# A two-layer graph kernel: own variances, inverse roots and edge places computed in another way, with a redrawn order of work

## The chip, the cores and the metric

The kernel runs on one core of a Trainium2 chip. The metric is the device time of one launch in microseconds: the median of several runs. Engines are named as in the profile: PE is TensorE (matmul; PEld is its weight load), DVE is VectorE, ACT is ScalarE, POOL is GpSimd, SP is the queue that issues DMAs. All engines work in parallel, each takes its own instructions strictly in the order in which the program issued them, and semaphores hold an instruction back until its inputs are there and its output buffer is free.

## The reference

There are 32 graphs of 512 nodes with 128 features. About one in sixteen of the entries of each 512 x 512 adjacency matrix is nonzero, and every node has an edge to itself. Two layers follow each other:

```python
# layer 0
adj1 = adj + eye(N)
d = rowsum(adj1) ** -0.5
x = layernorm(x + (d[:, :, None] * adj1 * d[:, None, :]) @ (x @ weight) + bias)
# layer 1
m_j = x @ W1[:D];  m_i = x @ W1[D:]
pre = m_j[:, None, :, :] + m_i[:, :, None, :] + b1       # for each pair i, j
msg = gelu(layernorm(pre, g1, be1), exact)
agg = einsum('bijo,bij->bio', msg, adj)
upd = layernorm(concat([x, agg]) @ W2 + b2, g2, be2)
x = layernorm(x + upd)
```

Only pairs (i, j) with a nonzero adjacency entry contribute to `agg`. The variance of a pair's `pre` (with centred weights) is a sum of a square in i, a square in j and twice a product, so that a matrix of all pair variances comes out of a few matmuls.

## The kernel before, in words

**Sparse lists.** The kernel splits each 512 x 512 matrix into 16 blocks of 128 x 128 and each block's rows into two halves of 64. `layer0` computes layer 0 and then `key`: the pair variance where there is an edge, and about -1e30 where there is none (the bf16 `mask` is added by a matmul with `ident_h`, L421). VectorE finds with MAX8 and FIND_INDEX8 the eight largest entries of each half row (`lists`); the first four of each become "slots", handled by gathers. `more` removes these eight (MATCH_REPLACE8) and looks once more in the whole block. What is left over beyond the slots goes to shared places: `counts` counts the leftovers of each row and takes running sums by a matmul (`po`, L620), so that each row's leftovers occupy places from `first` + 1 to `last`; `spots` makes one-hot matrices `sj` (rows x places) from these; `sending` multiplies the rows' data by them; `picks` reads out the node numbers and variances of the shared places.

**A node's edge to itself** is handled apart. `layer0` zeroes the diagonal of the transposed adjacency `a_t` (L325, GpSimd), so that the mask says "no edge" there. The variances of these own edges come from a separate matmul, `pown` (L392, with the summed weights `w1s`), a Square on ScalarE (`own_sq`, L395) and four column sums on TensorE (`psq` over `own_sq`, L399). `own_edges` uses them.

**Inverse roots.** `factors` needs, for the 128 slot entries of each row, the standard deviation `sd` and its inverse `r`. ScalarE takes the Sqrt (L548), VectorE the reciprocal (L551). Sqrt needs another activation table than Gelu, so two table loads stand around it. `sd` is transposed on TensorE (`psd`, L556), split into three bf16 parts (L477 to L483), written to DRAM (`sd_d`, L564) and read back as `sd_rows` (L837). For the shared places `picks` takes a power of -0.5 on GpSimd (`rsqrt`, L231).

**c3.** `parts` computes `ac` and splits its second half into three bf16 parts `c3`: each part is a cast on ScalarE (L451) followed by a subtraction on GpSimd (L449).

**Units.** The pairs are computed in 20 units for each batch, named (t, q): four slots t = 0..3 with four row blocks q each, and four units with t = 4, 5 for the shared places. The unit order is (0,0) ... (2,3), (3,0), (3,1), (4,0), (3,2), (4,1), (3,3), (5,0), (5,1). Each unit passes through these stages:

- `gathers` (L818): VectorE compares node numbers that a DMA has broadcast, which gives one-hot rows `s`; `turned` transposes them by DMA (L826) into `mt`.
- `pairs` (L855 to L875): TensorE multiplies the one-hots with `c3`, `sd_rows` and, for shared places, `sj`, into one of two PSUM buffers `u`.
- `sums` (L881): VectorE adds `ac` and frees that buffer; only for slots. Units of shared places are read by ScalarE from PSUM.
- `messages` (L914): ScalarE, eight Gelu instructions with scale `r`.
- `weights` (L897, L901): GpSimd multiplies `mt` with the adjacency values, giving `sw`.
- `aggregate` (L928, L938): TensorE adds up `sw` times message in PSUM.

**Order.** There is no scheduler: the program issues everything in an order written out by hand. A batch has 40 steps (two per unit). At each unit the loop at L1022 issues pairs for two units, the aggregate of earlier ones, weights, sums and messages; at every step `prepare` issues pieces of the side work. `PLAN` holds, for each phase, the step (relative to the batch's first unit) at which each of its pieces (up to the next `yield`) is issued; negative steps lie within the units of the batch before. Within one step the phases go in the order finish, layer0, lists, factors, more, counts, spots, sending, picks, parts, own_edges. So `layer0` of a batch begins 44 steps ahead of its first unit. SP issues DMAs in the same order. PSUM has three banks (`ps`) for all the side work. `a_nat` (the loaded adjacency) and `key` share one buffer, so the next load waits until `more` has read `key` for the last time.

**spots before.** For each of eight pairs of blocks VectorE compares 258 place numbers with `last` (`up_to`, L647: 1 where the place number is at most `last`), TensorE takes differences between neighbouring rows with the matrix `step_down` (`pj`, L660), and VectorE copies the result from PSUM to `sj` (L655).

Of the kernel before, what the change touches and what calls it, by code (L numbers as in the profile page):

```python
# [8 lines left out]
F32 = mybir.dt.float32  # L9
BF16 = mybir.dt.bfloat16  # L10
# [7 lines left out]
EPS = 1e-5  # L18
# [14 lines left out]
    "layer0": [-44, -41, -39, -39, -38, -36, -36, -34, -31, -31, -31, -31, -30, -30, -29, -25, -25, -25, -24, -23, -20, -18, -17, -13],  # L33
    "lists": [-20, -20, -20, -20, -18, -18, -18, -18, -17, -13, -13, -13, -13, -13, -13, -13, -12, -11, -10, -9, -8],
    "parts": [-18, -13, -13, -9, -9, -9, -8, -7, -7],
    "factors": [-11, -11, -10, -8, -7, -7, -7, -7, -6],
    "more": [-20, -18, -11, -10, -9, -9, -8, -8, -8, -6, -6, -6, -6, -6, -6, -6, -6, -6],
    "counts": [-5, -5, -4, -4, -4],
    "own_edges": [-6, -4, 21, 29],
    "spots": [-3, -2, -2, -1, 0, 2, 3, 4, 5, 8],  # L40
    "sending": [9, 9, 9, 9, 9, 9, 9, 9, 9, 9, 9, 9, 9, 9, 9, 9, 9],
    "picks": [13, 15, 16, 17, 18, 20, 22, 23, 23, 23, 23, 23],
    "finish": [43, 48, 49, 50, 55, 57, 59, 61, 62, 70, 74, 75, 77],
# [22 lines left out]
def sparse_path(ctx, tc, x, adj, w0, b0, w1, b1, g1, be1, w2, b2, g2, be2, out, most, flag):  # L66
# [66 lines left out]
    step_down = const.tile([P, P], BF16, name="step_down")  # L133
    nc.gpsimd.memset(step_down, -1.0)
    nc.gpsimd.affine_select(
        out=step_down, in_=step_down, compare_op=ALU.is_equal, fill=0.0, base=-1, pattern=[[1, P]],
        channel_multiplier=-1,
    )
    nc.vector.tensor_add(step_down, step_down, ident_h)
# [27 lines left out]
    w1s = const.tile([P, P], F32, name="w1s")  # L167
    nc.vector.tensor_add(w1s, w1c[:, 0, :], w1c[:, 1, :])
# [60 lines left out]
    def rsqrt(dst, src):  # L229

        nc.gpsimd.tensor_tensor(dst, src, power[:, 0:1].to_broadcast([P, src.shape[-1]]), ALU.pow)  # L231

# [36 lines left out]
    def layer0(b):  # L269
# [80 lines left out]
        )  # L350
        yield
# [39 lines left out]
        pc = bank(f"pown_{b}")  # L391
        nc.tensor.matmul(pc, w1s, x1t, start=True, stop=True)  # L392
        yield
        own_sq = node.tile([P, N], F32, tag="own_sq", name=f"own_sq_{b}")
        nc.scalar.activation(own_sq, pc, AF.Square, bias=b1c_col)  # L395
        pa = bank(f"psq_{b}")
        for k, sq in enumerate((asq, own_sq)):
# [96 lines left out]
    def lists(b):  # L494
# [8 lines left out]
        def half(n, h):  # L503
            i0 = (n % C) * P + h * HALF
            return key[:, n // C, i0 : i0 + HALF]
# [821 lines left out]
```

## Time and profile before

| | us |
|---|---|
| median of three runs | 3031.48 (3030.92 to 3032.12) |
| the profiled execution, in all | 3032.46 |
| its span, first to last instruction | 3030.8 |
| weight loads (PEld) busy in the span | 2379.5 |
| mean granted TensorE clock | 0.988 |
| HBM traffic over the span | 56 GB/s |

A line of a group reads: line, engine, operation, output<-input by the program's names, shapes, number of instructions | busy us, mean ns of one | idle time of the engine just before them and what ended it. A line of waits reads: what waited <- what ended the wait: total us, number of times, longest. A line of windows reads: stretch, its length, busy time (and number of instructions) of PE, PEld, DVE, ACT, POOL, granted clock, busy share of the DMA engines, GB/s. A line for one source line reads: operation, number, duration ns min/median/max. Busy times of pipelined instructions are counted once where they overlap, so the mean of one instruction times the count can exceed the busy time.

The order of work within one batch can be seen on GpSimd and VectorE around the end of a batch. This is the timeline of GpSimd there (start, length, instruction, number merged, idle before):

```profile
1444.18 1.17 POOL L897 TENSOR_TENSOR sw<-mt,a_t 128x512 f32<-128x512 bf16 x1
1445.64 0.67 POOL L614 TENSOR_TENSOR a_t<-a_t,over 128x256 f32<-128x256 f32 x1 [0.29 <-DVE over L604]
1446.28 0.86 POOL L615 TENSOR_SCALAR a_t<-a_t 128x256 f32<-128x256 f32 x1
...
1449.00 1.04 POOL L464 TENSOR_TENSOR own_u<-own_u,own_r 128x512 f32<-128x512 f32 x1
1450.12 1.27 POOL L465 TENSOR_TENSOR own_u<-own_u,be_row 128x512 f32<-128x512 f32 x1
1451.34 4.54 POOL L901 TENSOR_TENSOR sw<-mt,sent 128x512 f32<-128x512 bf16 x4
```

### The profile page before, as it was taken

How to read it: one execution, taken by the hardware profiler on the slowest of the kernel's cores; microseconds unless marked ns; L12 is line 12 of the kernel's file. 1: busy time of each engine (PE TensorE's matmuls, PEld its weight loads, DVE VectorE, ACT ScalarE, POOL GpSimd, SP SyncE). 2: the span in 40 equal slices, each digit the busy share in tenths (PEclk: the TensorE clock that was granted, in tenths of full speed). 3: DMA queues.
4: the chain of work that ended last, by engine and by line, in shares of the span. 5: the costliest groups of instructions: out<-in, count | busy, mean ns of one | idle time of the engine just before them, and what ended most of it. 6: DMA issues, size and time to landing. Idle time of an engine off the chain costs nothing. (4 is left out here: it accounts for less than half of the span.)

```text
span 3030.8 us, 96573 instructions
## 1 busy us (share of the span) xinstructions
PE 2844.0 (94%) x35522; PEld 2379.5 (79%) x35713; DVE 2423.9 (80%) x9803; ACT 2560.8 (84%) x7873; POOL 2065.0 (68%) x2525
## 2 busy tenths in 40 slices
PE   4999999999999999999999999999999999999996
PEld 2788878878778788788788788788787887887875
DVE  6777888777988777988778988778887779887782
ACT  2888888888888888888888888888888888888885
POOL 3576766676776677766667766767666767766765
PEclk7999999999999999999999999999999999999998
DMA  2344443444443444443445433444434444434441
GB/s 58 73 94 99 103 96 78 94 98 99 98 98 77 97 91 106 98 91 82 90 93 112 96 82 81 98 99 101 96 78 96 97 100 98 98 77 97 88 92 45
DMA packets 593025, 276.14 MB, mean 91 GB/s; under 512 B 456112, under 2 KB 576048, under 8 KB 592544
## 3 DMA queue, kind: packets, MB, share of 16 engines
q1 hardware_dynamic: 592320, 269.41, 40.5%
q8 instruction: 284, 4.65, 0.6%
q14 instruction: 197, 1.61, 0.2%
q0 software_dynamic: 224, 0.46, 0.1%
HBM read 155.45 MB, written 13.63 MB: 56 GB/s over the span
## 5 line engine op out<-in xcount | busy, mean ns | idle before, releaser
L914 ACT ACTIVATE m<-m,r 128x128 f32<-128x128 f32 x4096 | 1263.7, 392 | 18.6 <-DVE m L881 18.5
L881 DVE TENSOR_TENSOR m<-u,ac 128x1024 f32<-128x1024 f32 x512 | 609.6, 1211 | 329.8 <-PE u L863 319.2
L897 POOL TENSOR_TENSOR sw<-mt,a_t 128x512 f32<-128x512 bf16 x512 | 616.4, 1224 | 18.0 <-DMA mt<-s 15.1
L928 PE MATMUL agg<-m,sw 128*64 128x128 f32 x8192 | 515.3, 277 | 3.1 <-POOL sw L897 2.8
L928 PEld LDWEIGHTS agg<-m,sw 128*64 128x64 f32 x8192 | 444.6, 137 | 69.9 <-issue 34.2
L855 PEld LDWEIGHTS <-s 64*128 64x128 bf16 x12288 | 364.8, 94 | 140.0 <-issue 98.2
L870 PE MATMUL u<-ac,sj 128*128 128x128 f32 x2048 | 441.4, 297 | 24.4 <-DVE m L881 18.4
L855 PE MATMUL u<-c,s 64*128 64x128 bf16 x12288 | 433.4, 218 | 13.3 <-DVE s L818 13.1
L243 POOL TENSOR_SCALAR ve_l<-mv_l 128x4 f32<-128x4 f32 x96 | 33.7, 351 | 468.3 <-DVE mv_l L240 468.3
L870 PEld LDWEIGHTS u<-ac,sj 128*128 128x128 f32 x2048 | 325.1, 192 | 32.6 <-DVE m L881 25.7
L872 PE MATMUL u<-c,s 128*128 128x128 bf16 x3072 | 339.5, 220 | 0.0
L672 ACT COPY sent<-pl 128x328 f32<-128x328 f32 x512 | 221.2, 432 | 112.8 <-PE pl L676 57.2
L901 POOL TENSOR_TENSOR sw<-mt,sent 128x512 f32<-128x512 bf16 x256 | 291.4, 1163 | 12.2 <-PE agg L938 8.5
L676 PE MATMUL pl<-a_t,sj 128*128 128x164 f32 x2048 | 297.8, 304 | 0.8 <-ACT aggt L766 0.8
L676 PEld LDWEIGHTS pl<-a_t,sj 128*128 128x128 f32 x2048 | 286.4, 190 | 7.7 <-ACT sent L672 6.6
L914 ACT ACTIVATE m<-u,r_s 128x128 f32<-128x128 f32 x1024 | 272.2, 379 | 8.0 <-PE u L875 5.9
L938 PEld LDWEIGHTS agg<-m,sw 128*128 128x128 f32 x2048 | 236.4, 192 | 52.8 <-issue 51.6
L872 PEld LDWEIGHTS <-s 128*128 128x128 bf16 x3072 | 259.9, 99 | 12.1
L938 PE MATMUL agg<-m,sw 128*128 128x128 f32 x2048 | 250.6, 278 | 0.1
L513 DVE FIND_INDEX8 idx<-top,key 128x8 uint32<-128x64 f32 x1024 | 210.1, 218 | 0.0
L581 DVE MATCH_REPLACE8 key<-top,key 128x64 f32<-128x64 f32 x1024 | 205.8, 208 | 0.0
L863 PE MATMUL u<-be_d,sd_rows 64*128 64x512 bf16 x1024 | 195.5, 378 | 0.0
(214 smaller groups left out, 5641.8 us busy)
## 6 DMA issues: line engine op xcount, KB each, us to landing
raw<-idx_d SPq DMA_DIRECT2D x256, 256.5 KB
raw<-idx_ds SPq DMA_DIRECT2D x64, 513.0 KB
a_nat<-in_adj_dram SPq DMA_DIRECT2D x32, 1024.0 KB
sd_rows<-sd_d SPq DMA_DIRECT2D x768, 12.0 KB
xs<-in_x_dram SPq DMA_DIRECT2D x32, 256.0 KB
out_dram<-o_sb SPq DMA_DIRECT2D x32, 256.0 KB
sd_d<-sd_p SPq DMA_DIRECT2D x256, 12.0 KB
mt<-s SPq DMA_TRANSPOSE x192
```

The lines of the kernel that those rows point to most:

```text
L513: nc.vector.max_index(idx[:, n - 1, h, :], top[:, n - 1, h, :], half(n - 1, h))
L672: nc.scalar.copy(sent[:, n - 1], pt[:, : SHARED * WIDE].rearrange("p (k w) -> p k w", w=WIDE))
L676: nc.tensor.matmul(pt[:, k * WIDE : (k + 1) * WIDE], sj[:, n, k * P : (k + 1) * P], at[:, n, :], start=True, stop=True,)
L855: nc.tensor.matmul(pu[:, h, c, :], s[halved(h), c, q * P : (q + 1) * P], c3[halved(h), k, c, :], start=(c == 0 and k == 0), stop=False,)
L870: nc.tensor.matmul(pu[:, h, c, :], place, st["ac"][:, q_h, 0, :], start=(c == 0), stop=False)
L872: nc.tensor.matmul(pu[:, h, c, :], s[:, c, q_h * P : (q_h + 1) * P], c3[:, k, c, :], start=False, stop=False)
L881: nc.vector.tensor_tensor(u.rearrange("p h c d -> p (h c) d"), pu.rearrange("p h c d -> p (h c) d"), bcast(state[b]["ac"][:, q, 0, :], 2 * C),
L897: nc.gpsimd.tensor_tensor(sw, mt[:, :, q, :], st["a_t"][:, q, :, :P], ALU.mult)
L901: nc.gpsimd.tensor_tensor(sw, mt[:, :, q_h, :], a, ALU.mult)
L914: nc.scalar.activation(m[:, h, c, :], u[:, h, c, :], AF.Gelu, scale=r[:, k : k + 1])
L928: nc.tensor.matmul(agg[halved(h), c, :], sw[0][:, c, halved(h)], m[:, h, c, :], start=(begin and c == 0), stop=(end and c == C - 1),)
L938: nc.tensor.matmul(agg[:, c, :], sw[h][:, c, :], m[:, h, c, :], start=False, stop=(end and h == 1 and c == C - 1),)
```

## The change

1. *Own variances from the keys' diagonal.* `pown`, `own_sq`, `w1s` and the second set of `psq` columns go. GpSimd sets the mask's diagonal to 0, so that `key` holds the own edges' variances there; GpSimd then multiplies the diagonal blocks of `key` by the identity and writes -1e30 onto the diagonal; VectorE reduces the product to `own_v`. In `lists` and `more` the four diagonal blocks are taken last (`seq`).
2. *Inverse roots by Newton.* A new `inverse_root` on GpSimd: a first guess from the number's bits, then three Newton steps of four instructions. It replaces Sqrt and reciprocal in `factors` (there `sd` is then the variance times `r`) and the power in `picks`. The power stays in the layer norms, `own_edges` and the degrees.
3. *c copies on GpSimd.* The three casts to `c3` move from ScalarE to GpSimd.
4. *Places by two comparisons.* `step_down` and `pj` go. `sj` is now (place > `first`) * (place <= `last`), one scalar_tensor_tensor on VectorE for each block, from `places_1` and `up_to`.
5. *Positions redrawn.* All of `PLAN` changes. `layer0` has two pieces more, `spots` one less.

```diff
 PLAN = {
-    "layer0": [-44, -41, -39, -39, -38, -36, -36, -34, -31, -31, -31, -31, -30, -30, -29, -25, -25, -25, -24, -23, -20, -18, -17, -13],
-    "lists": [-20, -20, -20, -20, -18, -18, -18, -18, -17, -13, -13, -13, -13, -13, -13, -13, -12, -11, -10, -9, -8],
-    "parts": [-18, -13, -13, -9, -9, -9, -8, -7, -7],
-    "factors": [-11, -11, -10, -8, -7, -7, -7, -7, -6],
-    "more": [-20, -18, -11, -10, -9, -9, -8, -8, -8, -6, -6, -6, -6, -6, -6, -6, -6, -6],
-    "counts": [-5, -5, -4, -4, -4],
-    "own_edges": [-6, -4, 21, 29],
-    "spots": [-3, -2, -2, -1, 0, 2, 3, 4, 5, 8],
-    "sending": [9, 9, 9, 9, 9, 9, 9, 9, 9, 9, 9, 9, 9, 9, 9, 9, 9],
-    "picks": [13, 15, 16, 17, 18, 20, 22, 23, 23, 23, 23, 23],
-    "finish": [43, 48, 49, 50, 55, 57, 59, 61, 62, 70, 74, 75, 77],
+    "layer0": [-44, -44, -41, -41, -41, -41, -39, -38, -38, -38, -37, -37, -35, -33, -33, -32, -32, -32, -32, -32, -30, -28, -27, -27, -21, -15],
+    "lists": [-30, -30, -29, -28, -28, -28, -26, -26, -23, -20, -20, -20, -19, -19, -18, -18, -18, -16, -16, -16, -16],
+    "parts": [-23, -18, -13, -7, -6, -5, -5, -5, -3],
+    "factors": [-12, -12, -12, -11, -9, -9, -8, -7, -5],
+    "more": [-18, -15, -11, -11, -11, -10, -7, -7, -7, -7, -6, -5, -5, -5, -5, -5, -5, -5],
+    "counts": [-5, -4, -4, -4, -4],
+    "own_edges": [5, 5, 9, 22],
+    "spots": [-4, -4, -4, -4, -4, -4, -4, 2, 4],
+    "sending": [1, 2, 4, 4, 4, 4, 4, 4, 4, 4, 4, 4, 4, 4, 4, 4, 4],
+    "picks": [4, 5, 7, 11, 11, 16, 17, 19, 19, 21, 21, 23],
+    "finish": [44, 45, 45, 47, 48, 51, 51, 53, 57, 69, 74, 80, 80],
 }
...
+    places_1 = const.tile([P, SHARED * P], BF16, name="places_1")
+    nc.vector.tensor_copy(places_1, place_w.rearrange("p k e -> p (k e)")[:, : SHARED * P])
...
+    def inverse_root(dst, src, key):
+
+        width = src.shape[-1]
+        guess = small.tile([P, width], I32, tag=f"guess{width}", name=f"guess_{key}", bufs=1)
+        nc.gpsimd.tensor_scalar(guess, src.bitcast(I32), -0.5, 1597463007.0, ALU.mult, ALU.add)
+        y = guess.bitcast(F32)
+        z = small.tile([P, width], F32, tag=f"z{width}", name=f"z_{key}", bufs=1)
+        for k in range(3):
+            nc.gpsimd.tensor_tensor(z, y, y, ALU.mult)
+            nc.gpsimd.tensor_tensor(z, z, src, ALU.mult)
+            nc.gpsimd.tensor_scalar(z, z, -0.5, 1.5, ALU.mult, ALU.add)
+            nc.gpsimd.tensor_tensor(dst, y, z, ALU.mult)
+            y = dst
...
+        own_m = mask.rearrange(blocks, i=P)[:, own, :]
+        nc.gpsimd.affine_select(
+            out=own_m, in_=own_m, compare_op=ALU.not_equal, fill=0.0, base=0, pattern=[[0, C], [1, P]],
+            channel_multiplier=-1,
+        )
...
-        pc = bank(f"pown_{b}")
-        nc.tensor.matmul(pc, w1s, x1t, start=True, stop=True)
-        yield
-        own_sq = node.tile([P, N], F32, tag="own_sq", name=f"own_sq_{b}")
-        nc.scalar.activation(own_sq, pc, AF.Square, bias=b1c_col)
+        yield
         pa = bank(f"psq_{b}")
-        for k, sq in enumerate((asq, own_sq)):
-            for q in range(C):
-                nc.tensor.matmul(
-                    pa[:, k * C + q : k * C + q + 1], sq[:, q * P : (q + 1) * P], ones[:, :1], start=True, stop=True
-                )
+        for q in range(C):
+            nc.tensor.matmul(pa[:, q : q + 1], asq[:, q * P : (q + 1) * P], ones[:, :1], start=True, stop=True)
...
+        own_k = key.rearrange("p q (c i) -> p (q c) i", i=P)[:, own, :]
+        picked = node.tile([P, C, P], F32, tag="t1", name=f"own_p_{b}")
+        nc.gpsimd.tensor_tensor(picked, own_k, bcast(ident, C), ALU.mult)
+        nc.gpsimd.affine_select(
+            out=own_k, in_=own_k, compare_op=ALU.not_equal, fill=NEG, base=0, pattern=[[0, C], [1, P]],
+            channel_multiplier=-1,
+        )
+        yield
+        own_v = small.tile([P, C], F32, tag="own_v", name=f"own_v_{b}")
+        nc.vector.tensor_reduce(own_v, picked, AX.X, ALU.add)
+        st["own_v"] = own_v
+        yield
...
-            nc.scalar.copy(c3[:, k], rest)
+            nc.gpsimd.tensor_copy(c3[:, k], rest)
...
+        seq = st["seq"] = [n for n in range(C * C) if n % (C + 1)] + list(range(0, C * C, C + 1))
...
-            nc.gpsimd.tensor_scalar(by_c[:, h], top[:, h, :, :, :SLOTS], 0.0, None, ALU.max)
-        yield
-        nc.scalar.activation(sd, sd, AF.Sqrt, bias=eps_t, scale=1.0 / D)
+            nc.gpsimd.tensor_scalar(by_c[:, h], top[:, h, :, :, :SLOTS], 0.0, 1.0 / D, ALU.max, ALU.mult)
+        nc.gpsimd.tensor_scalar(sd, sd, EPS, None, ALU.add)
         yield
         r = small.tile([P, n_r], F32, tag="r", name=f"r_{b}")
-        nc.vector.reciprocal(r, sd)
+        inverse_root(r, sd, f"{b}")
+        yield
+        nc.gpsimd.tensor_tensor(sd, sd, r, ALU.mult)
...
-            if k >= 2:
-                nc.vector.tensor_copy(
-                    sj[:, 2 * k - 4 : 2 * k - 2, :], pt.pop(k - 2).rearrange("p (n e) -> p n e", n=2)
-                )
-            if 1 <= k <= n_pairs:
-                pt[k - 1] = bank(f"pj_{b}_{k}")
-                nc.tensor.matmul(pt[k - 1], step_down, up_to.pop(k - 1)[:, :, : SHARED * P], start=True, stop=True)
+            if k:
+                before = up_to.pop(k - 1)
+                for n in range(2):
+                    at_n = 2 * k - 2 + n
+                    nc.vector.scalar_tensor_tensor(
+                        sj[:, at_n, :], places_1, first[:, at_n : at_n + 1], before[:, n, : SHARED * P],
+                        ALU.is_gt, ALU.mult,
+                    )
...
         r = small.tile([P, n_r], F32, tag="r_s", name=f"r_s_{b}")
-        rsqrt(r, ve)
+        inverse_root(r, ve, f"s_{b}")
```

## The prediction

> **What bounds the kernel now.** I read first the busy shares and the slices, then the time by windows, then TensorE's list of waits, then the groups by shape.
>
> ```profile
> PE 2844.0 (94%) x35522; PEld 2379.5 (79%) x35713; DVE 2423.9 (80%) x9803; ACT 2560.8 (84%) x7873; POOL 2065.0 (68%) x2525
> ```
>
> ```profile
> 1402.80:1494.50 91.70, 88.17 (x1112) 73.96 (x1118) 75.48 (x306) 79.86 (x248) 64.26 (x78) 1.00 0.43 94
> ```
>
> The second line is one batch (the same matmul of two successive batches stands 91.69 us apart), with busy time in the order PE, PEld, DVE, ACT, POOL. TensorE works 88.2 of 91.7 us at full granted clock. The others have 12 to 27 us to spare. TensorE's idle time is 3030.8 - 2844.0 = 186.8 us: by windows 46.4 of it lie in the first 92 us and 29.1 in the last 91, so 111 us over the 31 periods between, 3.6 each. As 32 x 91.69 = 2934.1, the span is 32 periods and 96.7 us.
>
> ```profile
> PE po L620 <- DVE count_h L612: 42.3, 31, 1.6
> PE pj L660 <- DVE sj L655: 22.3, 32, 1.7
> PE u L870 <- DVE m L881: 18.4, 30, 0.8
> PE pconv L357 <- DVE sj L655: 15.2, 30, 0.8
> PE u L855 <- DVE s L818: 13.1, 1, 13.1
> ```
>
> These are TensorE's longest waits (total, times, longest). The first four come once in each batch; the last is the start of the program. So time is gained only by what leaves TensorE's queue or shortens its waits. Whatever the other engines gain or lose counts only where TensorE comes to wait for it.
>
> **TensorE loses work.**
>
> ```profile
> L660 PE MATMUL pj<-up_to,step_down 128*128 128x512 bf16 x256 | 83.9, 387 | 24.7 <-DVE sj L655 22.3 <-DVE up_to L647 1.9
> L399 PE MATMUL psq<-ones,own_sq 128*128 128x1 f32 x256 | 33.6, 253 | 0.5 <-ACT own_sq L395 0.4
> L392 PE MATMUL pown<-x1t,w1s 128*128 128x512 f32 x64 | 33.0, 598 | 0.0
> ```
>
> All three groups go: 83.9 + 33.6 + 33.0 = 150.5 us. With pj go the 24.7 us idle before it and pconv's 15.2 us for a pj bank: 39.9.
>
> The two other waits sit in one chain, from the sum of unit (3,3) on VectorE to count_h. In the trace that sum starts 2.5 us after its matmuls end, as VectorE is still in "more". In the new order fewer "more" steps stand between the sums, and the transpose of xs (0.6 us) goes ahead of po, but a gather compare (1.2 us) goes ahead of count_h. Between keeping 42.3 + 18.4 = 60.7 us and losing them, I take half off: -30.
>
> **ScalarE** loses the two table loads of a batch (41.1 + 41.1), Sqrt 12.9, own_sq 21.9 and the c3 casts 59.0: 176 us, to 2385 or 74.5 a batch. On a spare engine that is worth nothing by itself.
>
> **VectorE** loses the sj copies (174.0) and the reciprocal (29.5). It gains 512 scalar_tensor_tensor of 128x256 from two SBUF inputs, a form that the trace lacks. Bounds are 0.344 us (the 128x128 form, L364) and 0.741 (128x512, L415); the nearest is tensor_tensor 128x256 from SBUF, 0.418 (L698), so 213.5 us. The reduce of own_v is like L713, 686 ns x 32 = 22. Net +32: 2456, 76.7 a batch. Hidden, as long as it is not in the wrong place (below).
>
> **GpSimd** gains, per batch:
> - the mask's and key's diagonal selects, as L325: 2 x 0.64, and the product own_p, as L446: 1.27. Together 2.55.
> - roots of 128x128: 13 Newton instructions, the EPS addition and sd*r, so 10 tensor_tensor and 5 tensor_scalar. The row of 128 elements on 32 partitions is 0.417 (L481); tensor_scalar lies between 0.249 (32 elements, L727) and 0.857 (256, L615), by proportion 0.51. 4.2 + 2.55, and 15 gaps of 0.08 between dependent instructions: 7.95.
> - roots of 128x32: 9 x 0.253 + 4 x 0.249 + 13 x 0.08 = 4.4 in place of the power, 5.44 + 0.08: -1.1.
> - three c3 copies of 128x512. Bounds are 0.285 (128x128, L599) and 1.16 (L449); I take the one-input row of that size, L325: 3 x 0.64 = 1.9.
>
> Sum +11.3: 64.5 to 75.8 us. Bounds: every 128- and 512-wide addition at the 1.27 us of a 512-wide tensor_tensor gives +25, so 90; every one at the smallest rows +6.
>
> **Where this meets TensorE's path.** (a) psd, a transpose in TensorE's order, now waits for GpSimd's whole block of roots (2 x 0.44 for the maxima + 7.95 = 8.8 us after the last "top"), before only for one activation. TensorE has the sums of units (2,2) and (2,3), pidx, and the pairs of (4,0) and (3,2) in between: 1.9 + 0.4 + 3.8 + 1.3 = 7.4 us, and about 0.9 of (3,1). Behind psd stand all later pairs. I take 0.5 us x 32 = 16, between 0 and 2 us (64).
>
> (b) The heavier one. Seven of the nine steps of "spots" now stand in one place, step -4, so VectorE runs 14 up_to compares (two take 0.51) and 12 of the new instructions in a row, 3.6 + 12 x 0.375 = 8.1 us, and the sums of (0,0) and (0,1) are queued behind. ScalarE's gelu of (0,0) waits for that sum, and s (L334) is queued behind the gelu, and TensorE's pconv waits for s. Counted from po, without a hindrance, sum (0,0) ends at 0.4 + 8.1 + 1.2 = 9.7 us, half the gelu and s at 12.1; TensorE comes to pconv after 2 x 1.5 (agg), 2.4 (pa), 1.6 (pairs), 1.0 (psup), 0.6 (pl) and 2 x 2.0 (agg) = 12.6. No wait, but 0.5 us of margin. GpSimd has sums of weights for (5,0) and (5,1), the c3 copy and the starts in the same stretch, 7.7 us. And VectorE and GpSimd hold each other up in this trace:
>
> ```profile
> L604 DVE TENSOR_SCALAR over<-a_t x32: 274/1245/1254, 69.1 to 2913.0; 128x256 bf16<-128x256 f32 x32
> ```
>
> The one execution beside an idle GpSimd took 274 ns. The other 31 overlap L897 on GpSimd and took 703 to 1254: the typical one begins 63 ns after L897 and ends 0.14 us after it. The other way round, ve_l (L243) has a median of 221 ns but 650 at most, while VectorE runs the two-input L707. The old sj copy has one PSUM input and never lengthened (676 to 691 ns) over 215 overlaps with GpSimd. If each of the 7.7 us on GpSimd delays the new instructions, sum and s move to 19.8 and pconv waits 7.2 us. If GpSimd slips between the up_to compares, 0. I take 1.7 x 31 = 53, bounds 0 and 223.
>
> The Trainium skill, "SBUF — State Buffer", section "SBUF: two separate sides", speaks against this edit: an instruction on VectorE with two SBUF inputs and a GpSimd instruction that reads SBUF exclude each other for the whole instruction. It agrees with the 1245 against 274 above (there in a fast mode of one input); whether the new form does the same no row shows. Taken strictly it puts (b) at its upper bound, and the time near 3055.
>
> (c) The start: psd stands at 56.7 us, and TensorE then idles 13.1 us for the first gather. The roots add some 7 us on the way of sd and the c3 copies stand behind them, partly inside that gap: +5, between 0 and 13.
>
> (d) The next batch's load. SP issues xs and a_nat (L273, L275) behind eight sd_d and six sd_rows issues, 3.7 + 2.4 us; in the trace a_nat is issued 1.7 us before po and used by the first mask 4.7 us after it (6.5 us of landing), and the first transposes of a_nat come 7 us after po. In the new order those stand 3 us after po. But the last cast of sd comes some 12 us before po (9 in the trace), and the last "more" frees the buffer 4.5 us before it, so the load would be there at -4.5 + 6.5 = 2.0. I take 0; without that cover 1.7 x 31 = 53.
>
> **Sum**, against the profiled execution's span: 3030.8 - 150.5 - 39.9 - 30 + 16 + 53 + 5 = 2884.4. That execution took 3032.46 in all; the median of the three runs, 3031.48, stands 0.7 above the span. Forecast 2885, a period of 87.1 us.
>
> **The rivals.**
> - *Nothing new waits:* (a), (b), (c) at 0: 2885 - 74 = 2811. For it: the positions leave margins, and three engines keep 10 us a batch. Against it: 0.5 us of margin at pconv. 15%.
> - *GpSimd becomes a second bound* at its upper costs: 96.7 + 32 x 90 = 2977. For it: the new instructions are short, and each waits for the one before. Against it: the 32- and 256-wide rows fit my prices. 18%.
> - *Slower:* the mutual exclusion at step -4 in full. Place: the 12 new instructions between po and the sum of (0,0); price 7.2 us in each batch: 2885 - 53 + 223 = 3055. It turns the change to a loss from (3031.5 - 2832) / 31 = 6.4 us of wait. For it: the row of L604. Against it: VectorE's up_to compares, 3.6 us, can lie beside GpSimd's work. 9%.
> - My forecast 58%.
>
> **Range.** 2825 to 2975: it leaves out the best part of the first rival, a few per cent of the second and all of the third. Faster or slower means by over 0.2%, some 6 us, about what a measurement of this kernel can tell from no change. The forecast and the first two rivals are all faster, and near the third's turning point little lies within 0.2%: 0.89, 0.02, 0.09.
>
> **What would show it.** TensorE busy near 2694; pj, pown and the second psq gone; no table load in the batches; ScalarE near 2385. GpSimd near 2425; 128-wide Newton instructions of 0.4 to 0.5 us; if over 0.8, the second rival. Waits of pconv for s (L341 of the changed kernel), and the duration of the two-input instruction (L682): near 0.4 it is free, near 1.3 the exclusion holds. psd waiting for sd by over 1 us a batch makes (a) too small. The prediction is wrong in its root if TensorE's idle time in the middle rises above 8 us a batch.

## The result and the profile after

| | us |
|---|---|
| before, median | 3031.2 (3030.83 to 3032.12) |
| changed, median of four runs | 3152.71 (3148.41 to 3155.73) |
| ratio | 1.040, 95% interval 1.038 to 1.042 |
| the changed kernel's profiled execution, span | 3153.4 |

The change makes the kernel 4% slower; the forecast was 2885 us. The busy times of the changed kernel:

```profile
PE 2840.0 (90%) x35137; PEld 2381.2 (76%) x35137; DVE 2628.0 (83%) x10058; ACT 2394.2 (76%) x7650; POOL 2364.6 (75%) x3579
```

ScalarE came out nearly as forecast (2385), GpSimd a little lower (2425 forecast), VectorE 172 us higher (2456). TensorE was to fall to 2694 and did not; its idle time rose from 186.8 to 313.4 us. One period of the changed kernel by windows (stretch, length, busy time of PE, PEld, DVE, ACT, POOL, clock, DMA share, GB/s):

```profile
1465.40:1560.90 95.50, 88.15 (x1098) 73.98 (x1098) 81.77 (x314) 74.71 (x240) 73.62 (x112) 0.98 0.40 90
```

A period has grown by 3.8 us, and the granted clock in it is no longer 1.00. TensorE's longest waits:

```profile
PE pconv L369 <- ACT s L341: 113.4, 31, 4.5
PE u L880 <- DVE m L906: 63.2, 66, 6.4
PE pidx L543 <- ACT idx_h L537: 30.8, 34, 5.7
PE pa L305 <- DMA a_nat<-in_adj_dram: 18.3, 13, 4.4
PE psd L576 <- POOL sd L571: 18.0, 14, 9.9
PE pcs L408 <- ACT at L400: 13.7, 31, 0.4
```

The waits of po, of pj and of the shared units' u are gone, as hoped. In their place stands one that the forecast knew by name, pconv for s, and a few that it had no term for. The groups (line, engine, shapes, number | busy us, mean ns | idle before):

```profile
L682 DVE SCALAR_TENSOR_TENSOR sj<-places,first,up_to 128x256 f32<-128x256 bf16 x512 | 351.2, 725 | 0.0
...
L369 PE MATMUL pconv<-s,a_t 128*128 128x128 f32 x1024 | 174.0, 350 | 117.2 <-ACT s L341 113.4 <-POOL a_t L332 3.8
...
L717 DVE TENSOR_SCALAR rank<-sent,place_k 128x64 f32<-128x64 f32 x64 | 43.8, 728 | 195.7 <-ACT sent L697 195.7
```

pconv waits, and then its 32 matmuls of a batch are slower too (350 ns a piece, 280 before). The new two-input instruction takes 725 ns on average, where 375 to 418 were put. The timeline around step -4 of one batch (start, length, engine, line, number merged, idle before) shows how the one makes the other:

```profile
1517.59 1.10 DVE L671 TENSOR_SCALAR up_to<-places,last 128x258 bf16<-128x258 bf16 x4
...
1518.62 1.22 DVE L682 SCALAR_TENSOR_TENSOR sj<-places,first,up_to 128x256 f32<-128x256 bf16 x2
...
1519.52 5.26 POOL L926 TENSOR_TENSOR sw<-mt,sent 128x512 f32<-128x512 bf16 x4
1519.87 0.60 DVE L671 TENSOR_SCALAR up_to<-places,last 128x258 bf16<-128x258 bf16 x2
...
1520.39 2.06 DVE L682 SCALAR_TENSOR_TENSOR sj<-places,first,up_to 128x256 f32<-128x256 bf16 x2
...
1525.62 0.87 DVE L682 SCALAR_TENSOR_TENSOR sj<-places,first,up_to 128x256 f32<-128x256 bf16 x2
...
1530.64 2.34 DVE L906 TENSOR_TENSOR m<-u,ac 128x1024 f32<-128x1024 f32 x2
1531.89 1.28 ACT L939 ACTIVATE m<-m,r 128x128 f32<-128x128 f32 x4 [5.62 <-DVE m L906]
1533.07 1.11 ACT L341 ACTIVATE s<-psup,dinv 128x128 f32<-128x128 f32 x4
...
1533.56 5.44 PE L369 MATMUL pconv<-s,a_t 128*128 128x128 f32 x32 [4.30 <-ACT s L341]
```

VectorE is on places from 1517.6 to 1530.6 without a break. A pair of two-input instructions takes 0.87 us when GpSimd runs little ones, and 2.06 while GpSimd's four sums of weights run (themselves 5.26, before 4.54). The sum of (0,0) and (0,1), then the gelu, then s are queued behind, and pconv comes last. Its 5.44 us were 3.81 before. The windows there (columns as above) show why:

```profile
1528.00:1532.00 4.00, 1.26 (x12) 1.07 (x10) 4.00 (x6) 0.11 (x1) 3.66 (x5) 1.00 0.52 134
1532.00:1536.00 4.00, 2.44 (x13) 2.47 (x14) 3.50 (x6) 4.00 (x16) 1.27 (x2) 0.74 0.01 2
1536.00:1540.00 4.00, 4.00 (x43) 3.82 (x44) 0.89 (x4) 2.26 (x8) 0.62 (x1) 0.83 0.01 4
```

After the idle stretch the clock is granted at less than full.

For the account below I laid the sequence of TensorE's matmul groups of all middle batches over one another. Each entry is us per period from a group's first start to the next group's first start, so a wait counts with the group before it (pconv's with "agg"); "pt" are the transposes of x, xs and agg; the last column is the best kernel of the experiments.

```
                 before   after   one operand (e3)   best (e16)
pj                 2.08    0.00    0.00               0.00
pown, own psq      1.87    0.00    0.00               0.00
pt                 2.94    1.57    1.51               1.50
u, all kinds      32.25   34.44   34.29              32.65
agg               23.54   27.77   23.86              24.00
pconv              3.65    5.23    3.57               3.57
all else          25.43   26.46   26.45              26.46
period            91.75   95.47   89.68              88.19
```

### The profile page after: what moved, and what is told of

Read it like the earlier page. It is cut to its first block, busy times and chain, and to the rows that moved or that the text cites. A ratio compares the mean times of both kernels' runs of the same rounds, so it can differ in the third digit from the quotient of the medians.

```text
span 3153.4 us, 96745 instructions
## 1 busy us (share of the span) xinstructions
PE 2840.0 (90%) x35137; PEld 2381.2 (76%) x35137; DVE 2628.0 (83%) x10058; ACT 2394.2 (76%) x7650; POOL 2364.6 (75%) x3579
## 5 line engine op out<-in xcount | busy, mean ns | idle before, releaser
L922 POOL TENSOR_TENSOR sw<-mt,a_t 128x512 f32<-128x512 bf16 x512 | 603.3, 1189 | 40.7 <-DMA mt<-s 39.7
L953 PE MATMUL agg<-m,sw 128*64 128x128 f32 x8192 | 531.3, 278 | 4.1 <-POOL sw L922 3.7
L953 PEld LDWEIGHTS agg<-m,sw 128*64 128x64 f32 x8192 | 452.7, 137 | 93.9 <-POOL sw L922 33.0
L880 PE MATMUL u<-c,s 64*128 64x128 bf16 x12288 | 435.7, 218 | 67.6 <-DVE m L906 63.2
L682 DVE SCALAR_TENSOR_TENSOR sj<-places,first,up_to 128x256 f32<-128x256 bf16 x512 | 351.2, 725 | 0.0
L926 POOL TENSOR_TENSOR sw<-mt,sent 128x512 f32<-128x512 bf16 x256 | 314.0, 1251 | 14.2 <-PE agg L963 8.4
L250 POOL TENSOR_SCALAR ve_l<-mv_l 128x4 f32<-128x4 f32 x96 | 21.4, 223 | 392.7 <-DVE mv_l L247 390.1
L701 PE MATMUL pl<-a_t,sj 128*128 128x164 f32 x2048 | 304.3, 304 | 0.0
L369 PE MATMUL pconv<-s,a_t 128*128 128x128 f32 x1024 | 174.0, 350 | 117.2 <-ACT s L341 113.4
L369 PEld LDWEIGHTS pconv<-s,a_t 128*128 128x128 f32 x1024 | 168.8, 262 | 122.4 <-issue 108.1
```

The lines of the kernel that those rows point to most:

```text
L369: nc.tensor.matmul(o, a_t[:, mc, c, :P], s[:, mc, :], start=(mc == 0), stop=(mc == C - 1))
L682: nc.vector.scalar_tensor_tensor(sj[:, at_n, :], places_1, first[:, at_n : at_n + 1], before[:, n, : SHARED * P], ALU.is_gt, ALU.mult,)
L701: nc.tensor.matmul(pt[:, k * WIDE : (k + 1) * WIDE], sj[:, n, k * P : (k + 1) * P], at[:, n, :], start=True, stop=True,)
L880: nc.tensor.matmul(pu[:, h, c, :], s[halved(h), c, q * P : (q + 1) * P], c3[halved(h), k, c, :], start=(c == 0 and k == 0), stop=False,)
L922: nc.gpsimd.tensor_tensor(sw, mt[:, :, q, :], st["a_t"][:, q, :, :P], ALU.mult)
L926: nc.gpsimd.tensor_tensor(sw, mt[:, :, q_h, :], a, ALU.mult)
```

## The experiments

Each ratio is to the kernel before, run beside it (3031.6 to 3033.9), with its 95% interval. "P", "X" and "L" are the theories that e1 names; "A", later, is the theory that grew out of X, and it had to be mended on the way.

### Which part costs what

**e1: the changed kernel at the positions of before** (two pieces for the longer layer0, one less for spots).

```diff
-    "layer0": [-44, -44, -41, ... -27, -27, -21, -15],
+    "layer0": [-44, -41, -39, ... -18, -17, -13, -13, -11],
-    "spots": [-4, -4, -4, -4, -4, -4, -4, 2, 4],
+    "spots": [-3, -2, -1, 0, 2, 3, 4, 5, 8],
```

> The changed code with the positions of the kernel before (two pieces of layer0 added at -13 and -11, spots spread over steps -3 to 8, lists shifted slightly so that each block is there when read). Theory P (the redrawn positions did the harm): TensorE's wait of pconv for s falls from 113 us to under 20, the sums' wait under 30; 2870 to 2960 us. Theory X (the two-input instruction and GpSimd exclude each other, and that costs wherever it stands): the instruction keeps a mean near 0.7 us; 2960 to 3060. Theory L (too much work moved to GpSimd and VectorE): above 3060 whatever the positions.

3372.92 us, ratio 1.113 (1.111 to 1.115). The redrawn positions are 220 us better for the new code than the old ones. What costs here is a wait of 10 us in each batch:

```profile
PE psd L576 <- POOL sd L571: 311.4, 32, 10.4
```

**e5: parts 1 to 3, with the old places on TensorE, at the positions of before.**

```diff
-                    nc.vector.scalar_tensor_tensor(sj[:, at_n, :], places_1, ...)
+                pt[k - 1] = bank(f"pj_{b}_{k}")
+                nc.tensor.matmul(pt[k - 1], step_down, up_to.pop(k - 1)[:, :, : SHARED * P], start=True, stop=True)
```

> The first three parts of the change (own variances, Newton roots, c copies) with the places as before (differences on TensorE) and the positions of before. TensorE loses pown and the second psq, some 60 us by their spacing. Theories P and X: 2950 to 3000 us, as nothing of these parts stands in TensorE's way; psd waits under 1 us a batch. Theory L: GpSimd's added 11 us a batch make TensorE wait for psd and for sw; 3040 or more.

3301.78 us, ratio 1.089 (1.087 to 1.091); psd waits 310.9 us in 32 times.

**e7: as e5, with the roots of before too** (parts 1 and 3 alone).

```diff
-        inverse_root(r, sd, f"{b}")
+        nc.scalar.activation(sd, sd, AF.Sqrt, bias=eps_t, scale=1.0 / D)
+        nc.vector.reciprocal(r, sd)
-        inverse_root(r, ve, f"s_{b}")
+        rsqrt(r, ve)
```

> Parts 1 and 3 alone (own variances from the keys' diagonal, c copies on GpSimd), with the roots and the places of before and the positions of before. Theory A (the 310 us that psd waited under these positions are the Newton roots' own): psd waits under 32 us in all, and the own variances' matmuls take some 60 us of TensorE with them: 2950 to 3000 us. Rival (own variances on the keys' way, or the copies on GpSimd, make the lists or the roots late): psd or another product waits over 150 us, 3100 us or more.

3053.9 us, ratio 1.008 (1.006 to 1.009). psd's wait is 1.8 us, so it was Newton's. But the 60 us for pown and its psq did not show: by starts they take 1.87 us out of a period, while agg takes 1.80 more (25.34) and po's, u's and agg's waits grow (u for m 32.3 us, 18.4 before; agg for sw 10.5, before 2.8). GpSimd's added work makes its sums of weights later, as the wait for sw shows. All waits together grow by 1.0 us a period; the rest of agg's 1.80 is no wait, its matmuls start further apart, and no run says why. Forecast had been 2950 to 3000.

**e4: part 4 alone, at the positions of before.** The same hunks of part 4, spots as in e1.

> The kernel before with part 4 alone (places by two comparisons on VectorE), at the positions of before, its nine pieces at steps -3 to 8. Theory A: the second comparison is costly only where VectorE has no slack, in a burst beside GpSimd; spread out, it costs VectorE time but no TensorE wait, and pj goes with its waits (24.7 + 15.2 us) and some 56 us of TensorE: 2930 to 2990 us, L682's counterpart at 0.6 to 0.8 us mean, pconv waiting under 0.5 us a batch. Rival: the comparison excluded beside GpSimd makes VectorE late wherever it stands: 3050 us or more, u waiting for m over 100 us. Between the two neither stands alone.

3102.54 us, ratio 1.023 (1.021 to 1.025), L682's counterpart at 809 ns on average, u for m 63.6 us. A expected a gain: it fell here, the rival held. pconv does not wait (2.2 us). The dear instruction costs even when spread.

At the positions of before, then, parts 1 and 3 cost 21 us, Newton's roots 248 (e5 less e7), the places 71 (e1 less e5; 70 alone): together the 340 by which e1 is slower. None of the three gains there.

**e9 and e11: the changed kernel with part 4 undone; and with the roots undone too.** Redrawn positions, the code as in e5 and e7, ten pieces of spots:

```diff
-    "spots": [-4, -4, -4, -4, -4, -4, -4, 2, 4],
+    "spots": [-4, -4, -4, -3, -3, -2, -1, 0, 2, 4],
```

> The changed kernel with part 4 alone undone (places by one comparison and TensorE's difference again, ten pieces at steps -4, -4, -4, -3, -3, -2, -1, 0, 2, 4), all else as redrawn. Theory A (the second comparison of two SBUF operands is what the changed kernel loses by): pconv's wait for s falls from 113 to under 25 us, pj comes back with 84 us busy and some waits; from the 2972 us of the kernel with one comparison of one operand, plus pj's two us a batch and up to one of waits: 3035 to 3075 us, so 80 to 115 us under the changed kernel. Rival (places at step -4 are late whoever makes them): 3120 us or more, with pconv or pl waiting.

> As the kernel with part 4 undone, and the inverse roots undone too (square root on ScalarE, reciprocal on VectorE, power on GpSimd), the positions redrawn. Theory A (Newton's roots cost 250 us at the positions of before because psd is due too soon after the lists, and the redrawn positions give them that time): within 25 us of the kernel with part 4 undone. Rival (Newton's roots cost GpSimd time that is dear wherever they stand): this kernel is 60 us or more faster than that one.

e9: 3161.33 us, ratio 1.042 (1.040 to 1.044); e11: 3316.28, ratio 1.096 (1.092 to 1.099). In e9 pconv's wait for s fell as expected (2.6 us; another 11.2 are for the PSUM bank that the copy to sj frees), but pj came back dearer than in the kernel before, where 24.7 us were idle ahead of it:

```profile
L689 PE MATMUL pj<-up_to,step_down 128*128 128x512 bf16 x256 | 98.5, 405 | 72.2 <-DVE up_to L676 37.0 <-ACT x_t L302 31.0
```

So the undoing is no clean test of part 4: at step -4 the places are late by either way. In e11 both theories fell: the roots of before are 155 us worse at the redrawn positions. More than half of it shows behind one of VectorE's waits:

```profile
DVE r L575 <- ACT sd L572: 112.4, 32, 3.6
```

The reciprocal stands in the same step as ScalarE's square root, VectorE waits 3.5 us for it in each batch, and the sums behind it make u wait (80.8 us). Newton on GpSimd alone crosses no engine. The same part loses 248 us at one set of positions and wins 155 at the other.

### The places at step -4

**e3: the second comparison with one SBUF operand.**

```diff
-                    nc.vector.scalar_tensor_tensor(
-                        sj[:, at_n, :], places_1, first[:, at_n : at_n + 1], before[:, n, : SHARED * P],
-                        ALU.is_gt, ALU.mult,
+                    nc.vector.tensor_scalar(
+                        sj[:, at_n, :].rearrange("p (k e) -> p k e", k=3), places, first[:, at_n : at_n + 1],
+                        None, ALU.is_gt,
```

> The changed kernel with its positions, but sj is made by one comparison with one SBUF input (place > first); the second comparison's result is left out of sj. Theory X: the instruction takes under 0.45 us in mean beside GpSimd, the run of twelve at step -4 shortens from 13.0 to some 7.5 us, pconv's wait for s falls under 20 us; 3000 to 3060 us. Theory P: a run of 24 instructions ahead of the sum is too much in itself; pconv's wait stays above 60; above 3090. Theory L: gain under 30 us, as VectorE loses under 5 us a batch.

This kernel leaves the comparison with `last` out of sj, so it serves for its time alone. 2972.32 us, ratio 0.981 (0.979 to 0.982): 180 us less than the changed kernel. pconv waits 2.7 us and its matmuls are at 281 ns again. The second comparison in the changed kernel and here (three durations: least, median, most):

```profile
L682 DVE SCALAR_TENSOR_TENSOR sj<-places,first,up_to x512: 466/480/1495, 81.8 to 3057.9; 128x256 f32<-128x256 bf16 x171
...
L682 DVE TENSOR_SCALAR sj<-places,first x512: 459/469/482, 77.1 to 2875.6; 128x258 f32<-128x258 bf16 x171
```

Where GpSimd is idle beside them, both take 470 ns (median of 14 and of 22). So the edit takes away the hold, not a dearer operation; a mean of 725 ns with a median of 480 says that the hold falls on a part of the 512 only.

**e2: the changed kernel, pieces of spots one to a step.**

```diff
+    "spots": [-4, -3, -2, -1, 0, 1, 2, 3, 4],
```

> The changed kernel with one line of positions altered: the nine pieces of spots stand at steps -4 to 4, one each, in place of seven at -4. Theory P: sum (0,0) is no longer behind twelve two-input instructions, pconv's wait for s falls from 113 us to under 30, TensorE's clock stays at full there (pconv back from 174 us busy to about 125); 3010 to 3070 us. Theory X: mean of the two-input instruction still near 0.7 us, pconv's wait falls by no more than half; 3080 to 3120. Theory L: within 20 us of 3153.

3061.21 us, ratio 1.009 (1.007 to 1.011). pconv's wait falls to 6.4 us, but u now waits 104.5 us for m: the dear instruction moved, and holds up other sums.

**e6, e8 and e10: the first comparison into PSUM.** e6 at the changed positions; e8 with the first five picks later as well; e10 with the pieces spread, and both comparisons of a pair in one piece.

```diff
-                up_to[k] = node.tile([P, 2, n_places], BF16, tag="up_to", ...)
+                up_to[k] = bank(f"up_to_{b}_{k}").rearrange("p (n e) -> p n e", n=2)
```

> The changed kernel and its positions; only, the first comparison writes its result to PSUM, so that the second reads one operand from SBUF and one from PSUM; the same sum is computed. Theory A (two SBUF operands are held up by GpSimd's, and that makes the burst at step -4 late): the second comparison falls from 725 ns to 420 to 520 ns on average, pconv's wait for s from 113 us to under 25 us, and the time to 2960 to 3010 us, near the 2972 us of the kernel with one comparison of one operand. Rival (what made that one fast was the operation itself, or PSUM banks are now short): the comparison stays over 650 ns or TensorE waits for banks, 3060 us or more.

> As the kernel with the PSUM operand, and the first five picks at steps 8, 9, 10, 12 and 14 in place of 4, 5, 7, 11 and 11. If VectorE's wait for sent (rank at step 4, 196 us in all in the changed kernel) is what makes m late for u, u's wait for m falls from some 55 to under 25 us and the time by 25 to 60 us against that kernel: 2920 to 2970 us. If that wait of VectorE lies beside work that TensorE has in hand anyway, the two agree within 10 us.

> The changed kernel with the first comparison into PSUM, both comparisons of a pair in the same piece (so that VectorE holds one bank at a time and gives it back within the piece) and the pieces one to a step from -4. The same sum is computed. Theory A (second comparison at some 475 ns, no bank kept from TensorE): pa's wait for sj falls from 220 us to under 20 us, pconv's for s stays under 15 us, u's for m is under the 105 us of the kernel that only spread the pieces; 2960 to 3010 us. Rival (TensorE has too few banks even so, or VectorE's load near step 0 itself costs the time): pa or u waits over 100 us, 3040 us or more.

e6: 3300.32, ratio 1.088 (1.086 to 1.090). The two-operand instruction, one operand in PSUM, is no longer held up (three durations: least, median, most):

```profile
L684 DVE SCALAR_TENSOR_TENSOR sj<-places,first,up_to x512: 460/473/480, 83.6 to 3201.0; 128x256 f32<-128x256 bf16 x171
```

But of the three PSUM banks of the side work VectorE now keeps two, and TensorE waits for them:

```profile
PE pa L307 <- DVE sj L684: 220.3, 32, 7.8
PE pl L703 <- DVE sj L684: 39.9, 32, 5.2
```

e8 is worse still, 3368.25 (ratio 1.111, 1.109 to 1.113): u's wait for m rises from 13.9 to 36.2 us and agg's for sw from 3.7 to 15.8, the opposite of what was expected. e10: 3028.35, ratio 0.998 (0.997 to 0.999), pa still waits 37.9 us for a bank. The operand was mended, the banks took it back.

**e12 and e17: the same sum by two instructions with one SBUF operand each,** at the changed positions. A place's distance from the first one is written in bf16; its bits, read as uint16, are compared with the bits of the count, so a negative distance is a large number. e12 makes the distance by two operations into a tile with gaps; e17 by one, without gaps.

```diff
-                        places, last[...], None, ALU.is_le,
+                        places, first[...], 1.0, ALU.subtract, ALU.subtract,
...
-                    nc.vector.scalar_tensor_tensor(...)
+                    nc.vector.tensor_scalar(
+                        sj[:, at_n, :].rearrange("p (k e) -> p k e", k=3), before.bitcast(U16)[:, n, :, : n_places // 3],
+                        bits[:, at_n : at_n + 1], None, ALU.is_lt,
```

> The changed kernel and its positions, the same sum, by two instructions with one SBUF operand each: the place's distance from the first one (bfloat16), and that distance's bits read as an unsigned 16-bit number and compared with the bits of the count (a negative distance is then a large number). Theory A (the loss is the second SBUF operand): the second instruction takes 400 to 500 ns beside GpSimd as alone, pconv's wait for s is under 15 us, and the time is 2960 to 2990 us, the one of the kernel with one comparison of one operand. Rival (that kernel was fast because work was missing, or 258 columns of any instruction in a burst are too many): 3040 us or more.

> As the distance kernel at the changed kernel's positions, its first instruction with one operation (the first place plus one is made once a batch) and a result without gaps. Theory A: the first instruction comes to 330 to 400 ns as in the kernel with one comparison of one operand, the stretch at step -4 to 8.3 to 9.5 us, pconv's wait under 20 us, the time to 2960 to 3000 us. Rival (subtraction, not the form, makes that instruction long): it stays at 500 ns or more and the time at 3090 to 3130 us.

e12: 3111.66, ratio 1.028 (1.024 to 1.031); e17: 3077.2, ratio 1.014 (1.012 to 1.015). Neither comes to e3's 2972. The durations of e12:

```profile
L673 DVE TENSOR_SCALAR up_to<-places,first x512: 281/308/1329, 78.6 to 3000.7; 128x258 bf16<-128x258 bf16 x171
...
L685 DVE TENSOR_SCALAR sj<-up_to,bits x512: 456/466/477, 79.6 to 3004.7; 128x258 f32<-128x258 uint16 x171
```

and of e17:

```profile
L675 DVE TENSOR_SCALAR up_to<-places,second x512: 330/340/351, 79.2 to 2981.7; 128x258 bf16<-128x258 bf16 x171
...
L686 DVE TENSOR_SCALAR sj<-up_to,bits x512: 340/351/1418, 80.3 to 2984.5; 128x258 f32<-128x258 uint16 x171
```

In each kernel one instruction keeps its time within 7%, and the other, which has only one SBUF operand as well, is stretched to over four times. The stretched one is the faster form of its kind: alone it takes 293 ns where the steady form of the first instruction takes 340, and 342 where the steady form of the second takes 466. "Two SBUF operands" was too narrow a name for what is held up.

**e18: the changed kernel, two of the seven pieces moved to steps -2 and 0.**

```diff
+    "spots": [-4, -4, -4, -4, -4, -2, 0, 2, 4],
```

> The changed kernel, with two of the seven pieces at step -4 moved to -2 and 0; instructions and operands as they were. Theory A (all of the stretch of places at step -4 beyond some 9.5 us reaches TensorE, whatever makes it long): the stretch falls from 13.1 to some 9 us (18 of 26 instructions), pconv's wait for s from 113 to under 15 us, its product's 174 us back to under 130 us, and the time to 2980 to 3030 us. Rival (two SBUF operands cost TensorE wherever they stand, as in the kernel with pieces one to a step, 3061 us): u's wait for m grows to 100 us and the time is 3050 us or more.

3161.1, ratio 1.043 (1.041 to 1.044), pconv waits 124.6 us. The edit did not do what I took it to do: no sum stands on VectorE between steps -4 and 0, so the stretch stayed at 13.1 us. It rules nothing out.

The kernels together give the relation that the expectation named. "Stretch" is the median, over the middle batches, of VectorE's time from the first comparison after `first` to the last one before the next sum; the wait is pconv's for s, divided by 31 batches:

| | stretch, us | wait, us a batch | pconv, ns each |
|---|---|---|---|
| e16 | 7.7 | 0.1 | 280 |
| e3 | 8.3 | 0.1 | 281 |
| e14 | 8.4 | 0 | 280 |
| e2 | 8.9 | 0.2 | 278 |
| e17 | 11.4 | 2.5 | 323 |
| e12 | 12.3 | 2.8 | 332 |
| changed | 13.1 | 3.7 | 350 |

Up to some 9 us the stretch is hidden; beyond that pconv waits, in three kernels with three forms of instruction. It is not one for one: in the changed kernel the seven batches with a stretch of 11.7 us make pconv wait 0.7 to 2.1 us, the 23 with 13.1 us 3.7 to 4.5.

### The waits that the forecast did not price, and a better kernel

**e13, e14, e15: from e12.** e13 copies idx_h one step earlier; e14 also spreads the pieces; e15 is e13 with the first three picks later.

```diff
-    "lists": [... -18, -18, -18, -16, -16, -16, -16],
+    "lists": [... -18, -18, -18, -17, -16, -16, -16],
     e14:
+    "spots": [-4, -3, -2, -1, 0, 1, 2, 3, 4],
     e15:
-    "picks": [4, 5, 7, 11, 11, 16, ...
+    "picks": [6, 7, 8, 11, 11, 16, ...
```

> As that one, with the copy of idx_h one step earlier (-17 in place of -16) than its product. If the redrawn positions' same step for both is what makes TensorE wait for it (30.8 us, about 1 us a batch), that wait goes and the time falls by 15 to 40 us. Rival (ScalarE's copy at -17 holds up m there, or TensorE waits elsewhere instead): within 10 us of it.

> As that second one, with the pieces of the places one to a step from -4 to 4. If with one SBUF operand the burst at -4 is harmless, this brings nothing or costs up to 30 us (VectorE is then loaded up to step 4, where sent is made from the last places: pl waits for sj); if the burst still costs, it is 20 us or more faster.

> As the kernel with idx_h earlier, and the first three picks at 6, 7 and 8 in place of 4, 5 and 7. If VectorE's wait for sent at step 4 is what makes u wait for m (54.8 us with one comparison of one operand), that wait falls under 30 us and the time by 15 us or more; rival: the picks' later parts then crowd VectorE or GpSimd and the time stays within 10 us or rises.

e13: 3121.17, ratio 1.029 (1.026 to 1.031), no gain over e12: pidx's wait falls from 30.9 to 20.3 us, but agg then waits 15.4 us for m, the gelu of ScalarE, which makes the copy. The rival held. e14: 2989.71, ratio 0.986 (0.984 to 0.988), 131 us under e13. e15: 3080.99, ratio 1.016 (1.013 to 1.020), 40 us under e13, and u's wait for m goes from e13's

```profile
PE u L886 <- DVE m L912: 53.1, 65, 4.3
```

to e15's

```profile
PE u L886 <- DVE m L912: 7.4, 18, 4.3
```

So that wait was made by the picks at step 4, where VectorE stands waiting for `sent` (196.7 us in e13, 124.9 in e15) with the sums queued behind.

**e16: e17's instructions, the pieces spread, the first three picks later.**

> The distance kernel with its short first instruction, the pieces one to a step from -4 to 4, idx_h's copy at -16 again and the first three picks at 6, 7 and 8. If what each brought adds up (2990 us for the spread one, some 40 us by the picks, a few by the shorter first instruction): 2930 to 2965 us. Rival (u's wait for m is then VectorE's load around steps 0 to 4, which the picks don't change): 2975 us or more.

2927.36 us, ratio 0.965 (0.963 to 0.966), against the kernel before; 225 us under the changed one.

```profile
PE 2769.2 (95%) x34946; PEld 2327.0 (79%) x35137; DVE 2588.1 (88%) x10121; ACT 2392.9 (82%) x7650; POOL 2354.7 (80%) x3579
```

VectorE is busy for 40 us less than in the changed kernel, and the difference is mostly where its work stands.

## Why the prediction was wrong

By periods, the forecast's terms that recur in each batch make -4.7 us (its sum over 32, without the start), measured were +3.7. The difference of 8.4, times 32, is the 268 us.

**The removal (-150.5 - 39.9, or -5.95 a period): mechanism right, size a little off.** pj, pown, the own psq and the waits in "pt" took 5.3 us out of a period. A group's busy time holds pipeline overhang that lies beside its neighbours: by starts the three groups were 3.95 us a period, 126 us, not 150.5. Missing: 0.6 a period, 20 us.

**Term (b), pconv behind the places (+53): the step that failed first.** Place, chain and mechanism were as the prediction put them; the margin was better than put (stretch of about 9 us, forecast 8.6). The size failed: "8.1 us" for the stretch holds for a form that is not held up (e3: 8.3) and not for this one (13.1). (The instruction alone takes 470 ns, not the 375 put, but so does e3's, so that is not what makes the difference.) The wait is 113.4 us. And the prediction had no price for what comes after a wait: pconv's matmuls at less than full clock, 1.6 us more a period. Together 5.1 a period in place of 1.7: 3.5, or 110 us. e3, which has the same positions without the hold, shows it: it is 180 us faster.

**"I take half off: -30", and nothing else: the second failed step, as dear.** The waits of po and of the shared u did go. But the forecast looked for new waits only where the code changed, and four came with the redrawn positions: u for m 63.2 us behind the picks at step 4 (shown by e13 against e15, in e12's code), pidx 30.8 (7.6 before), pa 18.3 (5.1), pcs 13.7. With what else is spread over u, agg and the rest of the table, 4.4 us a period or 140 us stand against the forecast. Only about half of that is waits: outside pj's and pconv's a middle period holds 2.1 us of them before and 3.7 after, where the forecast had them fall by 0.4. The other half is no wait: the same matmuls start further apart (agg's take 22.9 us a period before and 23.7 after, waits left out). e16 takes back 1.8 of u's 2.2 and has 2.0 us of waits a period; what remains there, 1.9 us a period over all rows, is of the second kind, and no run explains it.

**(a), psd for the roots (+16): within its bounds, the size in part by luck.** Of the 18.0 us one wait of 9.9 lies at the start; the batches have 8.1, half of what was put. e1 and e5 show how narrow it was: at the positions of before the same roots cost 10 us a batch. **(c), the start (+5): right within its bounds;** the span beyond 32 periods is 98.3 us, before 94.8 by the same measure. **(d), the load (0):** pa's wait grew by 13 us.

**The rivals.** The one of a loss, at 9%, named place and mechanism, and asked 6.4 us of wait a batch before the sign turns. The wait came to 3.7, and the sign turned all the same: the removal and the second failed step were 160 us short already (e3, where pconv hardly waits, stands 140 us above the 2832 that the forecast's sum gives without (b)), and the wait brought 50 us of lost clock with it. So the chance failed through the sum: 6.4 was worked out as if all else held. GpSimd as a second bound did not come (74 us of work in a period of 95). And the prediction's own sign of being wrong in its root, TensorE idle for over 8 us a batch, did not show though it was wrong: 95.50 less 88.15 is 7.4, as matmuls at less than full clock count as busy. (In its price of the 128x32 roots the terms add up to 4.3, not 4.4; that changes nothing.)

**The rule that spoke against the edit.** The Trainium skill, "SBUF — State Buffer", section "SBUF: two separate sides", which the prediction weighed and put half aside, holds in this case: the two-input instruction takes 466 to 479 ns on an idle GpSimd and up to 1495 beside it, and with one operand in PSUM it never passes 480. The same section names a second kind that excludes GpSimd, instructions in a two-port mode, and that fits e12 and e17. By "VectorE: DVE Perf Modes", section "What auto-detection actually checks", an instruction runs in such a mode when its single source and its destination lie in SBUF and their outermost dimensions are both even or equal; the forms that were stretched here (gaps alike on both sides; no gaps on both sides) meet that, and the steady ones (gaps on one side only) do not. No view names the mode that an instruction ran in, so this is a reading of the durations.

## What to carry to other kernels

Price an instruction that two engines can hold up at its held duration, as soon as many of them stand in a row ahead of something that TensorE waits for; and ask how long a stretch may be before it shows, not only what it costs on average. A part of a change has no price of its own: the Newton roots lost 248 us at one set of positions and won 155 at another. When a change redraws the order of work, go through every product of TensorE in the new order, also those that the change does not touch.

## What the runs showed of the hardware

- *A wait of TensorE of a few microseconds was mostly, not always, followed by half the clock.* In the changed kernel pconv's 32 matmuls take 3.84 us after each of the six waits of up to 1.8 us, and 5.3 to 6.7 us after each of the 26 others, of which one is of 2.07 us and the rest are of 3.06 and more. The trace records the granted clock at 0.5 in 25 intervals (the first 120 and the last 90 us left out), each 3.41 or 6.83 us long; e3 has none there. But a wait of 2.30 us for pa passed without it, and so did six of the 25 waits of 2.6 to 3.4 us in e17, and three of 2.4 and one of 3.67 us in e12. And e2 has 16 such intervals, though no wait of TensorE in the same stretch is longer than 2.2 us: at each stand two waits of u, in 15 cases one of 1.3 to 1.7 and one of 1.4 us, 2.45 us apart. So the length of a single wait does not settle it. The Trainium skill, "TensorE: Matmul & The Clock Gate", section "What's actually happening", gives windows of about 3.4 us that run freely, which agrees with the length of the intervals; that waits shorter than one window suffice is what these traces show.
- *The faster form of an instruction can be the slower one.* e12's first instruction takes 293 ns on an idle GpSimd, and 542 on average in the kernel; the form with gaps on one side only takes 340 always.
- *A buffer in PSUM lifts the hold and costs banks:* 460 to 480 ns for all 512, and 220.3 us of TensorE's wait for pa.
